# The filling of a scan pipeline: where the weights' means stand, which PSUM banks are used, and who computes chunk 11's taps

## The chip, the core and the metric

The kernel runs on one core of a Trainium2 chip. A core has five engines that run side by side and wait for each other by semaphores: TensorE (PE, matrix products), VectorE (DVE), ScalarE (ACT), GpSimd (POOL) and SyncE (SP, which here only issues DMA transfers). Each engine works through its own list of instructions in the order in which the program wrote them. The metric is the device time of one execution in microseconds, the median of several.

## What is computed

The input `x` has 2 images of 768 channels by 64 x 64 positions. Two layers follow each other, each added to its input. The change touches only the first layer, and of that only the start:

```python
x = x + mamba(_gn(x), ...)             # layer 0
x = x + attention(_gn(x), ...)         # layer 1

# layer 0
x  = hs @ in_proj_w.T                  # 768 -> 1536 channels
xs = conv3x3_depthwise(x) + conv_b
xs = xs * sigmoid(xs)                  # SiLU: "activations" below
dt, Bs, Cs = split(xs @ x_proj_w.T)
delta = softplus(dt @ dt_w.T + dt_b)
dA, dBu = exp(delta * A), delta * u * Bs
states = scan(dA, dBu)                 # along the 4096 positions, 4 states per channel
y  = sum_n(states * Cs) + D * u
y  = (y - mean) * rsqrt(var) * ln_g + ln_b
out = y @ out_proj_w.T
```

The last normalisation is folded into the output weights: each row of `out_proj_w.T` is multiplied by `ln_g` of its channel, and the mean of all the scaled rows is taken off. The kernel does that once, at its start, and keeps the result (`wo_dr`) in device memory.

## The kernel before

**Tiling.** The 1536 inner channels are 12 chunks of 128 (`KI`), the positions 16 tiles of 512 (8 per image, `NI` in all). The work of layer 0 is a list of 192 items (`NQ0` = 16 tiles x 12 chunks). One call of `step(g)` (L1162) writes out, in a fixed order, one item's worth of every stage. The stages run at different offsets: step g does the input projection of item n = g + 17 (`in_proj`), the convolution's taps of item a = g + 15 (`taps_dve`, `AHEAD` = 15), the scan of item g, and the output projection that lies 12 items behind (`out_proj`, `BEHIND`). The order is written by hand: the call stands inside `tc.manual_schedule()`, so each engine meets its instructions in just the order of the code.

**The filling.** Before the first scan (g = 0) there are 17 steps, g = -17 to -1, in which only the front stages run. The loop at L1333 counts sixteen of them as v = 0 to 15 (so n = v and a = v - 2), and the step g = -1 follows in the main loop. I call them step 0 to step 16, by n. Below, "projection 7" is `in_proj(7)`, that is step 7.

What one filling step v holds, engine by engine and in this order:

- SP: load the weights of projection v + 2 (`load_wi`, four buffers), one or two pieces of image 1 for its group statistics (`gn_load`), and later tiles of x.
- PE: one image row before the tile (`row0`, only for the first twelve), then the projection (`in_proj`, twelve matrix instructions into one PSUM bank), then what is appended at the end of the step (one tap by PE, `taps_pe`; x_proj of four chunks, `x_proj_pair`).
- DVE: the taps of chunk v - 2 (`taps_dve`, L436), one `scalar_tensor_tensor` each, into a PSUM accumulator `acc`; the last one writes the slot `u`. Then the pieces' statistics.
- ACT: copy of the row (L339), in every fourth step four SiLUs with a table load before and after (`silu`, L443), the centre tap of chunk v - 1 which starts its accumulator (`tap_act`, L390), the copy of projection v to the buffer `xs` (`in_proj_evict`, L364 to L367), the normalisation of the next tile (`norm_x`, L307), the products of two taps that are added by DMA (`taps_act`, L402).
- POOL: issues the two accumulating DMAs that add those tap products (`taps_dma_sum` L408, `taps_dma` L414).

Of the nine taps of a chunk the centre is ACT's, taps 0 and 2 go by DMA in three chunks of four, and in the filling's chunks 3, 7 and 11 tap 1 goes by PE instead, through a diagonal matrix (`diag`, L385, `taps_pe`, L422), and no tap by DMA. What remains is DVE's: six taps or seven.

**Buffers that order the work.** There is one accumulator bank (`psC`, "acc"), so the centre tap of chunk a + 1 waits until DVE has finished chunk a. There are two `xs` buffers, so the copy of projection n waits until DVE has finished chunk n - 2. The projections share one bank (`psA`), except the odd ones from 12 on (`po0`), so a projection waits for the copy of the one before it. The `u` slots come from a first-in first-out list of 46.

**The output weights.** `wg` holds all twelve chunks of `out_proj_w.T`, loaded in steps 2 to 5. Behind step 7 `out_weights_rows` (L256) multiplies them with `ln_g` and `ln_b` on PE, and behind step 8 `out_weights_mean` (L269 to L273) makes the mean row and the bias. From step 8 on each chunk is scaled by ACT (L276), the mean is taken off by POOL or DVE (L277), and one step later SP stores it (L280). The scale is written behind everything else of its step on ACT, and the subtraction likewise on its engine.

**The end of the filling.** x_proj of the tile's last four chunks comes in step 14, its two halves are added and copied in step 15 (`x_halves`, `x_sum`, `x_dbl`), and B and C go to device memory and come back spread over all partitions (`load_bc`, L470) in step 16. The softplus of the first two chunks and the exponentials of the first are ACT's in step 16. `bc`, `s`, the two `da` buffers and the `tm` buffers lie in a pool (`late`) that takes over the space of the pool with `wg`.

Of the kernel before, what the change touches and what calls it, by code (L numbers as in the profile page):

```python
# [14 lines left out]
P = 128  # L15
# [4 lines left out]
NS = 4  # L20
# [24 lines left out]

DMA_TAPS = ((0, 2, 6), (0, 2, 6), (0, 2, 6), (0, 2))
PE_TAPS = ((), (), (), (1, 7))
FILL_DMA_TAPS = ((0, 2), (0, 2), (0, 2), ())  # L50
FILL_PE_TAPS = ((), (), (), (1,))

AHEAD = 15
BEHIND = 12
# [13 lines left out]
def both_layers(  # L68
# [174 lines left out]


    def out_weights_load(wg, k):
        nc.sync.dma_start(wg[:, k : k + 3, :], out_wT[k * P : (k + 3) * P, :].rearrange("(k p) m -> p k m", p=P))

# [2 lines left out]
    def out_weights_rows(wg, rows):  # L252
        gb = psO.tile([P, 512], F32, tag="po0", name="pgb")
        for k in range(KI):
            for j in range(KM // 2):
                nc.tensor.matmul(  # L256
                    gb[32 * j : 32 * j + 2, :MG], pc[:, k, PC_G : PC_B + 1], wg[:, k, j * MG : (j + 1) * MG],
                    start=(k == 0), stop=(k == KI - 1),
                )
        for j in range(KM // 2):  # L260
            nc.scalar.copy(rows[32 * j : 32 * j + 2, :], gb[32 * j : 32 * j + 2, :MG])

    def out_weights_mean(rows, wmean, pick):
        pb = psS.tile([P, 512], F32, tag="st", name="pbo")
        wm = [psO.tile([P, 512], F32, tag=f"po{e}", name=f"pwm{e}") for e in range(2)]
        for j in range(KM // 2):
            for e in range(2):
                m = 2 * j + e
                nc.tensor.matmul(pb[:, m : m + 1], rows[:, e * P : (e + 1) * P], pick[:, j, P : P + 1], start=True, stop=True)  # L269
            nc.tensor.matmul(wm[j // 2][:, j % 2 * MG : (j % 2 + 1) * MG], pick[:, j, :P], rows, start=True, stop=True)  # L270
        nc.scalar.copy(wmean[:, : 2 * MG], wm[0])
        nc.scalar.copy(wmean[:, 2 * MG :], wm[1][:, :MG])
        nc.scalar.copy(bias_o, pb[:, :KM])  # L273

    def out_weights_scale(wg, wmean, k, engine):
        nc.scalar.activation(wg[:, k, :], wg[:, k, :], AF.Copy, scale=pc[:, k, PC_G : PC_G + 1])  # L276
        engine.tensor_sub(wg[:, k, :], wg[:, k, :], wmean)  # L277

    def out_weights_store(wg, k):
        nc.sync.dma_start(  # L280
            wo_dr[:, k // 3, :, k % 3, :].rearrange("q p m -> p q m"), wg[:, k, :].rearrange("p (q m) -> p q m", m=2 * P)
        )

    us, deltas, dus, sqs, tms = {}, {}, {}, {}, {}
# [58 lines left out]
    def in_proj(n):  # L343
        i, c, b, t = where(n)
        nn = TL if t < NT - 1 or b + 1 < NB else TL - W
        w = wis.pop(n)
        if KI <= n < AHEAD + 2 and n % 2:
            pa = psO.tile([P, 512], F32, tag="po0", name=f"pa{n}")
        else:
            pa = psA.tile([P, 512], F32, tag="psa", name=f"pa{n}")  # L350
        for k in range(KM):
            nc.tensor.matmul(pa[:, :nn], w[:, k, :], xts[i, k][:, :nn], start=(k == 0), stop=(k == KM - 1))  # L352
        pas[n] = pa
        give_w(w)
        if c == KI - 1:
            for k in range(KM):
                give(xts.pop((i, k)))
# [15 lines left out]


    def dma_taps(a):
        return (DMA_TAPS if a >= AHEAD else FILL_DMA_TAPS)[a % 4]

    def pe_taps(a):
        return (PE_TAPS if a >= AHEAD else FILL_PE_TAPS)[a % 4]

    def diag(a):
        c = a % KI
# [3 lines left out]
        dgs[a] = dg  # L386

    def tap_act(a):
        acc = psC.tile([P, 512], F32, tag="acc", name=f"acc{a}")
        nc.scalar.activation(  # L390
            acc.rearrange("p (h w) -> p h w", w=W), xs_bufs[a % 2][:, 1 : 1 + TR, 1 : 1 + W], AF.Copy,
            scale=pc[:, a % KI, PC_W + 4 : PC_W + 5],
        )
        accs[a] = acc
# [735 lines left out]
    with tc.manual_schedule():  # L1130
# [31 lines left out]
        def step(g, prep=None):  # L1162
# [46 lines left out]
            if 0 <= a + 1 < NQ0:  # L1209
                diag(a + 1)  # L1210

            do_silu = g % 4 == 1 and 0 < a <= NQ0
            do_soft = g % 2 == 1 and 0 <= g + 1 < NQ0
            if do_silu:
                nc.scalar.preload_act_table_set(SILU_SET)
                for q in range(4):
                    silu(a - 4 + q)
            if do_soft:
                nc.scalar.preload_act_table_set(SOFTPLUS_SET)
                softplus_pair(g + 1)  # L1220
            if do_soft or do_silu:
                nc.scalar.preload_act_table_set(EXPLN_SET)
            if 0 <= a + 1 < NQ0:
                tap_act(a + 1)
# [22 lines left out]
                    norm_x1(0, d[1] + 1, k)  # L1247
            if 0 <= a + 1 < NQ0 and dma_taps(a + 1):
                taps_act(a + 1)
            if 0 <= g - 3 < NQ0:  # L1250
                square(g - 3)

# [55 lines left out]
                prep()  # L1308
            if do_silu:
                for q in range(0, 4, 2):  # L1310
                    x_proj_pair(a - 4 + q)
            if v == len(by_step) + 1:
                gn_aggregate(1)
                norms[g + 2] = gn_finish(1)
# [5 lines left out]
                norms[g + 2][0][0]()  # L1320

        with tc.tile_pool(name="l0st", bufs=1, side="right") as sp:
            wg = sp.tile([P, KI, DM], F32, name="wg")
            rows = sp.tile([P, MG], F32, name="gb_rows")
            nc.vector.memset(rows, 0.0)
            wmean = sp.tile([P, DM], F32, name="wmean")
            pick = sp.tile([P, KM // 2, P + 1], F32, name="pick")
            nc.sync.dma_start(pick, pick_in)

            first = -AHEAD - 2  # L1330
            ready_w = {8: (0,), 9: (1, 2), 10: (3,), 11: (4, 5), 12: (6, 7), 13: (8, 9), 14: (10,), 15: (11,)}
            prep = {7: lambda: out_weights_rows(wg, rows), 8: lambda: out_weights_mean(rows, wmean, pick)}
            for v in range(AHEAD + 1):  # L1333
                if 2 <= v < 6:
                    out_weights_load(wg, 3 * (v - 2))
                step(first + v, prep.get(v))
                if v == 0:
                    nc.scalar.activation(neg_a, pc[:, :, PC_A : PC_A + NS], AF.Exp)
                    nc.scalar.mul(neg_a, neg_a, -1.0)
                for k, engine in zip(ready_w.get(v, ()), (nc.gpsimd, nc.vector)):  # L1340
                    out_weights_scale(wg, wmean, k, engine)
                for k in ready_w.get(v - 1, ()):
                    out_weights_store(wg, k)
            for k in ready_w[AHEAD]:
                out_weights_store(wg, k)

        late = right.enter_context(tc.tile_pool(name="l0l", bufs=1, side="right"))
        bc = late.tile([P, 2 * NS, TL], F32, name="bc")

        ysum = late.tile([P, 3, TL], F32, name="ysum")  # L1350
        tm_bufs = [late.tile([P, TL], F32, name=f"tm{j}") for j in range(5)]
        das = [late.tile([P, NS, TL + 1], F32, name=f"da{j}") for j in range(2)]
        for da in das:
            nc.gpsimd.memset(da[:, :, 0], 0.0)
        s = late.tile([P, NS, TL + 1], F32, name="s")
        for g in range(-1, NQ0 + 2):
            step(g)
        right.close()

# [199 lines left out]
```

## Time and profile before

| | us |
|---|---|
| median of 3 runs | 3741.39 (3737.32 to 3745.57) |
| the profiled execution, its own time | 3742.55 |
| its span, first to last instruction | 3740.6 |

| stretch of the profiled execution, us | length | PE busy | DVE busy | ACT busy | POOL busy |
|---|---|---|---|---|---|
| 0 to 212.09 (up to the first scan) | 212.09 | 151.92 | 147.03 | 92.58 | 40.70 |
| 212.09 to 361.77 (scan, no output projection yet) | 149.68 | 104.75 | 144.16 | 125.03 | 81.74 |
| 361.77 to 2700 (all stages) | 2338.23 | 2268.69 | 2231.61 | 1993.16 | 1348.41 |
| 2700 to the end (layer 1) | 1040.60 | 1021.55 | 345.06 | 354.45 | 305.27 |

A busy time near the length of its stretch marks an engine that hardly waits there. The profile gives busy times per stretch, the groups of instructions by line, a timeline of each engine with the idle time before an instruction and what ended it, and a list of who waited for whom.

### The profile page before, as it was taken

Reading aid. Unit: us, or ns where it says so; the run is one execution under the profiler, and the core shown is the slowest. Engines: PE = TensorE matmul, PEld = TensorE weight load, DVE = VectorE, ACT = ScalarE, POOL = GpSimd, SP = SyncE. Lnnn points to the kernel's source line nnn. Section 1 sums busy time; section 2 is a strip of 40 time slices with the busy share of each in tenths; the row PEclk is TensorE's granted clock in tenths of the full one; section 3 lists DMA queues with packets and bytes.
Section 4 is the critical chain, followed back from the end, with each engine's and each line's share of the span. In section 5 each row is a group of like instructions: output and inputs, shape, how many; then the busy total and the mean of one; then the engine's idle time right before and its main releaser. Section 6 shows DMA issues by size and latency. Waiting matters only on the chain. (4 is left out here: it accounts for less than half of the span.)

```text
span 3740.6 us, 37806 instructions
## 1 busy us (share of the span) xinstructions
PE 3546.9 (95%) x11098; PEld 1763.4 (47%) x11098; DVE 2867.9 (77%) x2614; ACT 2565.2 (69%) x4988; POOL 1776.1 (47%) x1809
## 2 busy tenths in 40 slices
PE   5877999999999999999999999999999999999999
PEld 3422333333333333333343333333346658886688
DVE  7699999999999999999999999997721362224522
ACT  2588888888888988888889888887633541244221
POOL 0245565555655555555555655554443314320232
PEclk9988999999999999999999999999999999999999
DMA  9677898889989899898889988897666628764487
GB/s 353 176 177 147 188 205 185 201 190 212 202 187 201 184 212 201 190 210 175 201 200 199 205 181 202 187 213 175 145 195 181 206 79 271 250 214 127 150 270 245
DMA packets 379725, 737.93 MB, mean 197 GB/s; under 512 B 44240, under 2 KB 116880, under 8 KB 375424
## 3 DMA queue, kind: packets, MB, share of 16 engines
q0 software_dynamic: 145632, 269.03, 42.1%
q1 hardware_dynamic: 233888, 466.49, 38.0%
q8 instruction: 90, 1.47, 0.2%
q14 instruction: 115, 0.94, 0.1%
HBM read 440.96 MB, written 60.03 MB: 134 GB/s over the span
## 5 line engine op out<-in xcount | busy, mean ns | idle before, releaser
L352 PE MATMUL pa<-u,w 128*128 128x512 f32 (+1 forms) x2304 | 1046.1, 604 | 19.3 <-ACT carry L367 14.7
L578 PE MATMUL po<-u,w 128*128 128x512 f32 x2256 | 1013.4, 599 | 16.9 <-DVE u L590 16.9
L514 DVE TENSOR_TENSOR_SCAN s<-da,s 128x2052 f32<-128x2052 f32 x192 | 851.1, 4433 | 19.5 <-ACT u L307 0.5
L352 PEld LDWEIGHTS pa<-u,w 128*128 128x128 f32 x2304 | 433.3, 193 | 617.6 <-issue 488.7
L578 PEld LDWEIGHTS po<-u,w 128*128 128x128 f32 x2256 | 420.1, 190 | 596.1 <-issue 549.4
L501 POOL TENSOR_TENSOR ysum<-da 128x1024 f32<-128x1024 f32 x192 | 384.6, 2003 | 588.4 <-DVE da L521 465.4
L436 DVE SCALAR_TENSOR_TENSOR acc<-xs,pc,acc 128x512 f32<-128x512 f32 x741 | 558.4, 754 | 41.5 <-PE acc L422 11.5
L489 ACT ACTIVATE da<-dl,neg_a 128x512 f32<-128x512 f32 x768 | 489.6, 713 | 0.0
L512 DVE TENSOR_TENSOR s<-du,bc 128x2048 f32<-128x2048 f32 x192 | 439.0, 2286 | 57.1 <-POOL du L493 55.4
L408 POOL DMA_DIRECT2D tm<-tm x309 | 267.9, 867 | 439.9 <-ACT tm L402 380.6
L521 DVE TENSOR_TENSOR da<-s,bc 128x2048 f32<-128x2048 f32 x192 | 440.1, 2292 | 6.3
L508 POOL DMA_DIRECT2D u<-ysum x384 | 378.5, 1249 | 4.5 <-issue 2.7
L390 ACT ACTIVATE acc<-xs,pc 128x512 f32<-128x512 f32 x192 | 132.3, 689 | 286.3 <-DVE u L436 285.0
L402 ACT ACTIVATE tm<-xs,pc 128x512 f32<-128x512 f32 x486 | 317.1, 717 | 3.6 <-DMA tm<-tm 3.0
L493 POOL TENSOR_TENSOR du<-dl,u 128x512 f32<-128x512 f32 x192 | 243.8, 1270 | 0.0
L414 POOL DMA_DIRECT2D u<-tm x177 | 205.1, 1159 | 53.6 <-issue 36.4
L861 PE MATMUL po_p<-v,w 128*128 128x256 f32 x672 | 171.9, 380 | 1.4 <-ACT po_p L958 1.4
L861 PE MATMUL po_p<-u,w 128*128 128x256 f32 x624 | 159.6, 379 | 0.0
L436 DVE SCALAR_TENSOR_TENSOR u<-xs,pc,acc 128x512 f32<-128x512 f32 x192 | 143.6, 748 | 9.5 <-DVE acc L436 0.4
L861 PE MATMUL acc_p<-u,w 128*128 128x256 f32 x556 | 143.7, 382 | 4.1 <-DMA w<-woutP 2.9
L477 PE MATMUL pz<-xd,dt_w 48*128 48x512 f32 x384 | 112.6, 664 | 36.5 <-DVE gs_x L193 14.9
L806 POOL TENSOR_TENSOR v<-u 128x256 f32<-128x256 f32 x21 | 15.7, 758 | 276.7 <-ACT u L824 262.5
(284 smaller groups left out, 4970.3 us busy)
## 6 DMA issues: line engine op xcount, KB each, us to landing
u<-ysum POOLq DMA_DIRECT2D x384, 256.0 KB, 5.8
tm<-tm POOLq DMA_DIRECT2D x309, 256.0 KB, 4.5
w<-in_wP SPq DMA_DIRECT2D x192, 384.0 KB, 5.0
w<-wo_dr SPq DMA_DIRECT2D x192, 384.0 KB, 4.8
u<-x SPq DMA_DIRECT2D x263, 256.0 KB, 4.8
w<-s_dr_p SPq DMA_DIRECT2D x288, 192.0 KB, 4.0
u<-tm POOLq DMA_DIRECT2D x177, 256.0 KB, 5.8
bc<-bc_dr SPq DMA_DIRECT2D x32, 1024.0 KB, 6.9
```

What stands on the lines that cost most here:

```text
L352: nc.tensor.matmul(pa[:, :nn], w[:, k, :], xts[i, k][:, :nn], start=(k == 0), stop=(k == KM - 1))
L402: nc.scalar.activation(tm.rearrange("p (h w) -> p h w", w=W), xs[:, dy : dy + TR, dx : dx + W], AF.Copy, scale=pc[:, c, PC_W + j : PC_W + ...
L408: nc.gpsimd.dma_start(tms[a][0], tms[a][q], accum_op=ALU.add)
L436: nc.vector.scalar_tensor_tensor(dst, xs[:, dy : dy + TR, dx : dx + W], pc[:, c, PC_W + j : PC_W + j + 1], acc, ALU.mult, ALU.add)
L489: nc.scalar.activation(das[g % 2][:, n, 1:], deltas[g], AF.Exp, scale=neg_a[:, c, n : n + 1])
L501: nc.gpsimd.tensor_add(ysum[:, 0 : 2 + g % 2 : 1 + g % 2, :], da[:, 0:2, 1:], da[:, 2:4, 1:])
L508: nc.gpsimd.dma_start(us[g], ysums(g, n), accum_op=ALU.add)
L512: nc.vector.tensor_mul(s[:, :, 1:], dus.pop(g).unsqueeze(1).to_broadcast([P, NS, TL]), bc[:, :NS, :])
L514: nc.vector.tensor_tensor_scan(sf, das[g % 2].rearrange("p n l -> p (n l)"), sf, 0.0, ALU.mult, ALU.add)
L521: nc.vector.tensor_mul(das[g % 2][:, :, 1:], s[:, :, 1:], bc[:, NS:, :])
L578: nc.tensor.matmul(po[e], w[:, kk, e * P : (e + 1) * P], us[i * KI + k], start=(k == 0), stop=(k == KI - 1))
L861: nc.tensor.matmul(dst, half[:, k, :], tiles[blocks[seq[i][0]][:3]][what][k], start=(start and k == 0), stop=(k == KH - 1), skip_group_che ...
```

## The change

1. **Banks.** In the filling the accumulators alternate between two banks (`psC` "acc" and `psS` "st"), and every odd projection goes to the bank "po1".
2. **Taps.** In the filling chunks 3 and 7 are treated like the others (taps 0 and 2 by DMA). Chunk 11 has all eight taps by DVE. No tap goes by PE and no diagonal is made.
3. **First activations.** The SiLUs of chunks 0 to 3 and 4 to 7 move from the steps with a = 4 and 8 to those with a = 5 and 9 (steps 7 and 11), and there behind everything else of ACT. Those of chunks 8 to 11 stay where they are.
4. **Means.** `out_weights_rows` and `out_weights_mean` both come at the end of step 12. Scaling follows in steps 12 to 15 (3, 4, 3, 2 chunks). POOL subtracts for 9 chunks in the same step, DVE for 3 chunks one step later.
5. **Four buffers and the order of the late pool.** `wg` is four tiles of three chunks. The late pool is laid out anew, so that `da0` and the `tm` buffers of step 16 no longer overlap `wg`, and `bc` overlaps only its first two tiles. `da1` is cleared behind step 16.

```diff
-FILL_DMA_TAPS = ((0, 2), (0, 2), (0, 2), ())
-FILL_PE_TAPS = ((), (), (), (1,))
+FILL_DMA_TAPS = (0, 2)
...
     def out_weights_mean(rows, wmean, pick):
-        pb = psS.tile([P, 512], F32, tag="st", name="pbo")
-        wm = [psO.tile([P, 512], F32, tag=f"po{e}", name=f"pwm{e}") for e in range(2)]
+        wm = psZ.tile([P, 2, 512], F32, tag="pz", name="pwm")
+        pb = wm[:, 1, MG : MG + KM]
...
-    def out_weights_scale(wg, wmean, k, engine):
-        nc.scalar.activation(wg[:, k, :], wg[:, k, :], AF.Copy, scale=pc[:, k, PC_G : PC_G + 1])
-        engine.tensor_sub(wg[:, k, :], wg[:, k, :], wmean)
+    def out_weights_scale(wg, k):
+        w = wg[k // 3][:, k % 3, :]
+        nc.scalar.activation(w, w, AF.Copy, scale=pc[:, k, PC_G : PC_G + 1])
+
+    def out_weights_sub(wg, wmean, k, engine):
+        w = wg[k // 3][:, k % 3, :]
+        engine.tensor_sub(w, w, wmean)
...
-        if KI <= n < AHEAD + 2 and n % 2:
-            pa = psO.tile([P, 512], F32, tag="po0", name=f"pa{n}")
+        if n < AHEAD + 2 and n % 2:
+            pa = psO.tile([P, 512], F32, tag="po1", name=f"pa{n}")
...
     def dma_taps(a):
-        return (DMA_TAPS if a >= AHEAD else FILL_DMA_TAPS)[a % 4]
+        return DMA_TAPS[a % 4] if a >= AHEAD else FILL_DMA_TAPS if a != KI - 1 else ()
     def pe_taps(a):
-        return (PE_TAPS if a >= AHEAD else FILL_PE_TAPS)[a % 4]
+        return PE_TAPS[a % 4] if a >= AHEAD else ()
+    def silu_of(a):
+        if a < KI:
+            return {5: 0, 9: 4}.get(a)
+        return a - 4 if a % 4 == 0 and a <= NQ0 else None
...
-        acc = psC.tile([P, 512], F32, tag="acc", name=f"acc{a}")
+        bank, tag = (psS, "st") if a < AHEAD and a % 2 == 0 else (psC, "acc")
+        acc = bank.tile([P, 512], F32, tag=tag, name=f"acc{a}")
...
-            do_silu = g % 4 == 1 and 0 < a <= NQ0
+            first4 = silu_of(a)
+            do_silu = first4 is not None
...
+            if do_silu and a >= KI:
+                silus()
...
             if 0 <= a + 1 < NQ0 and dma_taps(a + 1):
                 taps_act(a + 1)
+            if do_silu and a < KI:
+                silus()
+                nc.scalar.preload_act_table_set(EXPLN_SET)
...
-            wg = sp.tile([P, KI, DM], F32, name="wg")
...
+            wg = [sp.tile([P, 3, DM], F32, name=f"wg{q}") for q in range(KI // 3)]
-            ready_w = {8: (0,), 9: (1, 2), 10: (3,), 11: (4, 5), 12: (6, 7), 13: (8, 9), 14: (10,), 15: (11,)}
-            prep = {7: lambda: out_weights_rows(wg, rows), 8: lambda: out_weights_mean(rows, wmean, pick)}
+            scaled_w = {12: ((0, 1), (2,)), 13: ((3, 4, 5), (6,)), 14: ((7, 8), (9,)), 15: ((10, 11), ())}
+            def means():
+                out_weights_rows(wg, rows)
+                out_weights_mean(rows, wmean, pick)
...
-                step(first + v, prep.get(v))
+                step(first + v, means if v == 12 else None)
...
-                for k, engine in zip(ready_w.get(v, ()), (nc.gpsimd, nc.vector)):
-                    out_weights_scale(wg, wmean, k, engine)
-                for k in ready_w.get(v - 1, ()):
+                for k in sum(scaled_w.get(v, ((), ())), ()):
+                    out_weights_scale(wg, k)
+                for k in scaled_w.get(v, ((), ()))[0]:
+                    out_weights_sub(wg, wmean, k, nc.gpsimd)
+                for k in scaled_w.get(v - 1, ((), ()))[1]:
+                    out_weights_sub(wg, wmean, k, nc.vector)
+                for k in sum(scaled_w.get(v - 1, ((), ())), ()):
                     out_weights_store(wg, k)
...
-        bc = late.tile([P, 2 * NS, TL], F32, name="bc")
-        ysum = late.tile([P, 3, TL], F32, name="ysum")
-        tm_bufs = [late.tile([P, TL], F32, name=f"tm{j}") for j in range(5)]
-        das = [late.tile([P, NS, TL + 1], F32, name=f"da{j}") for j in range(2)]
-        for da in das:
-            nc.gpsimd.memset(da[:, :, 0], 0.0)
+        ysum = late.tile([P, 3, TL], F32, name="ysum")
+        bc = late.tile([P, 2 * NS, TL], F32, name="bc")
         s = late.tile([P, NS, TL + 1], F32, name="s")
-        for g in range(-1, NQ0 + 2):
+        da1 = late.tile([P, NS, TL + 1], F32, name="da1")
+        tm_bufs = [late.tile([P, TL], F32, name=f"tm{j}") for j in (0, 3, 1, 2, 4)]
+        tm_bufs = [tm_bufs[j] for j in (0, 2, 3, 1, 4)]
+        das = [late.tile([P, NS, TL + 1], F32, name="da0"), da1]
+        nc.gpsimd.memset(das[0][:, :, 0], 0.0)
+        step(-1)
+        nc.gpsimd.memset(das[1][:, :, 0], 0.0)
+        for g in range(NQ0 + 2):
             step(g)
```

## The prediction

> **What bounds the kernel.** I begin with the busy times per stretch (columns: stretch, length, then busy time and instructions of PE, PEld, DVE, ACT, POOL, then the TensorE clock granted, DMA share, GB/s).
>
> ```profile
> 100.00:120.00 20.00, 18.16 (x113) 7.78 (x111) 13.24 (x19) 10.25 (x19) 3.71 (x5) 1.00 0.76 190
> 160.00:180.00 20.00, 12.86 (x25) 5.35 (x24) 14.06 (x16) 6.28 (x11) 5.37 (x4) 0.83 0.72 197
> 240.00:260.00 20.00, 13.85 (x30) 5.81 (x31) 19.61 (x12) 16.89 (x32) 10.66 (x11) 0.83 0.81 158
> 440.00:460.00 20.00, 20.00 (x52) 8.03 (x51) 19.69 (x11) 19.92 (x41) 9.25 (x10) 1.00 0.98 228
> ```
>
> From 440 on PE is full: it is the bound of the long stretch. From 240 to 260 DVE is full. At 160 nobody is: an order of waits is the bound. The change touches only the last kind, before the first scan. DVE does that scan in its timeline here:
>
> ```profile
> 208.55 2.34 DVE L436 SCALAR_TENSOR_TENSOR acc<-xs,pc,acc 128x512 f32<-128x512 f32 x3 [5.10 <-ACT tm L402]
> 210.92 0.75 DVE L436 SCALAR_TENSOR_TENSOR u<-xs,pc,acc 128x512 f32<-128x512 f32 x1
> 212.09 2.29 DVE L512 TENSOR_TENSOR s<-du,bc 128x2048 f32<-128x2048 f32 x1 [0.42 <-DMA bc<-bc_dr]
> ```
>
> From 212.09 DVE idles for 5.5 us in 149.68, then PE takes over as bound at 361.77 and idles for 69.5 in 2338. So **what counts is when the multiplication at 212.09 starts**; whatever it gains, the end gains. The list of waits (100 to 420 us; total, times, longest) says what holds the filling:
>
> ```profile
> ACT acc L390 <- DVE u L436: 47.2, 18, 7.4
> DVE wg L277 <- ACT wg L276: 20.8, 4, 7.9
> PE acc L422 <- ACT acc L390: 11.8, 2, 7.1
> PE pa L352 <- ACT carry L367: 8.7, 6, 3.0
> DVE acc L436 <- PE acc L422: 8.1, 1, 8.1
> ```
>
> The first line is the single accumulator bank, the second DVE standing before a scaling that ACT reaches late, the third and fifth the tap by PE, the fourth the projections' single bank.
>
> **How I work it out.** I follow the engines' lists step by step; an instruction starts when the one before it has gone and what it needs has ended (plus 0.05 to 0.1 us, as between the rows). Pitches from the timelines: on PE a row 1.3, a projection 5.2 (its end 0.15 later), a pair of x_proj 0.93; on DVE a tap 0.79 (six: 4.7), a piece 0.6, a subtraction 2.1; on ACT a centre tap 0.62, a projection's copy 0.8, two tap products 1.2, four SiLUs with both table loads 5.2, a normalisation 0.7, a scaling 0.84, a softplus pair with its loads 3.9, four exponentials 2.5.
>
> At full clock these rules put the old kernel's first scan at 210.3, 1.8 too early. The clock is missing:
>
> ```profile
> 149.88 7.11 PE L352 MATMUL pa<-u,w 128*128 128x512 f32 x12 [1.96 <-ACT carry L367]
> 157.84 5.42 PE L352 MATMUL pa<-u,w 128*128 128x512 f32 x12 [0.84 <-ACT carry L367]
> 170.40 2.07 PE L422 MATMUL acc<-xs,dg 128*128 128x512 f32 x2 [7.14 <-ACT acc L390]
> ...
> 189.64 5.42 PE L352 MATMUL pa<-u,w 128*128 128x512 f32 x12
> ```
>
> In PE's timeline (start, length) the same twelve instructions take 7.11 behind an idle spell and 5.42 without, and the tap 2.07 instead of the 1.02 of step 8. The Trainium skill ("TensorE: Matmul & The Clock Gate", "What's actually happening") says that PE falls to half clock after an idle window of some 3.4 us and returns after a busy one. With windows of 3.4 us, one under half busy halving the next, the old first scan comes at 212.0. The rule isn't always kept: projection 15, at 189.64, takes 5.42 although PE had idled 2.69 before the x_proj ahead of it. I use it, because it speaks against the change, as seen below.
>
> **The banks.** Projections 3 to 7 no longer wait for the copy before them; row and projection follow each other every 6.5 us, as 61.60 to 68.09 already shows. DVE needs 5.3 or 5.9 per step and starts each chunk as the last one ends, since its centre tap was made meanwhile. Projection 7 starts at 101.9 instead of 109.61. That includes 5 us from the SiLUs of step 6, now gone from there.
>
> **The taps.** Chunks 3 and 7 lose a tap on DVE (0.8 each) and a PE tap, and gain two products on ACT (1.2) and two accumulating DMAs; chunk 11 gains a DVE tap (0.8) and loses the PE tap, whose wait of 7.14 at 170.40 goes. All but that lies in slack. The added DMAs fall where the DMA share is above 1.0 until 100 us. The skill ("Trainium Kernel Development and Optimization", "Key Constraints") says that all queues share the same 16 engines; the trace agrees: tap DMAs landed after 7 to 9 us there and after 3.5 later. POOL passes them one behind another, so u of chunk 3 lands at 110 to 113.6, and its SiLU would start at 112.4: 0 to 1.2 lost. I take 0.
>
> **The SiLUs last.** They begin in step 7 behind ACT's own work, at 109.2. But x_proj is at the end of PE's step and needs them: PE stands from 107.3 to 112, and row and projection 8 are queued behind. Projection 8 starts at 115.4 at full clock. In step 11 it is the same: PE stands from 141 to 147, and projection 12 is late. Both gaps hold a whole window, so by the rule x_proj and some of the projection run at half clock: 1 to 2 us in step 8 and 1 to 2 more in step 12. Without the rule these cost 0.
>
> **The means.** The weights' products with gain and bias (5.3) and the means (2.6) go from behind steps 7 and 8, where PE waits anyway, to behind projection 12, in the path. ACT copies between them (1.1), so projection 13 starts 9.2 after the end of 12, and ACT can't reach the centre tap of chunk 12 before the means are copied: DVE idles about 10 us there. This gives back most of what the first steps won.
>
> **Scalings and stores.** ACT has 12 scalings as before, now all in its fullest steps. DVE's subtractions come a step later and no longer wait (20.8 before). From the end of projection 13 ACT hardly waits, and I add it up: copy, products, four scalings 5.3; SiLUs, centre tap, copy, products, three scalings 10.3; halves, centre tap, x_dbl with its wait for PE, copy, products, two scalings 6.6; diagonals, softplus, centre tap, copy, products, exponentials 9.5. From 171.9 that ends at 203.6 (now 210.98). POOL's last subtraction ends at 197.5 (old: 203.43). SP then stores, loads one weight and asks for B and C at 198.5 (old: 206.38). Of this 2.0 is the wait for the last stores' landing, which `bc` no longer has. Landing takes 5.7 as now. The clearing of `da1` on POOL adds a wait for the last store, until 200.2, and du of item 0 is behind it; but that waits for the products of step 16 until 201 anyway.
>
> | start of | trace | old by the rules | new |
> |---|---|---|---|
> | projection 7 | 109.61 | 109.4 | 101.9 |
> | projection 8 | 121.63 | 121.2 | 116.7 |
> | projection 12 | 157.84 | 157.4 | 151.9 |
> | projection 13 | 172.27 | 171.7 | 166.6 |
> | projection 16 | 199.92 | 199.3 | 191.5 |
> | load of B and C | 206.38 | 206.3 | 198.5 |
> | first scan's multiplication | 212.09 | 212.0 | 204.2 |
>
> **The sum:** 204.2 - 212.1 = -7.9 us (the windows' phase moves it from 7 to 8.6). At full clock throughout it is 200.8, or -11.3. Against the profiled execution's 3742.55 that makes 3734.7; the median of the runs is 1.2 lower, so I say 3733.5. A measurement of this kernel can tell about 0.2% from no change, that is 7.5 us: my forecast lies just beyond that edge.
>
> **Rivals.**
>
> *Full clock (0.18).* The waits of 5 us don't bring half clock, as before projection 15. First scan near 201, time 3730.
>
> *The waits eat most of it (0.24).* The tap DMAs hop along POOL at 9 us each; if they still do at chunk 3, u lands 3 us after its SiLU is due, and PE waits with ACT. With one further cold window at step 12 and one at step 15, 5 of the 7.9 go: 3738.5. For it: the SiLU of chunk 2 waited 3.48 for such a DMA. Against it: the new SiLUs come a step later.
>
> *The long loop pays (0.10).* The four slots more that chunks 3 and 7 take turn the list of 46 slots, so every later tile lies in other slots. If a slot were then asked for before its last reader is through, PE would wait in each step. PE idles 0.38 us per step in the loop now; 0.085 more in 180 steps is 15.4, from where the kernel is slower than before beyond the edge. With 0.1 it is 3751.5. Against it: the list is first in, first out, and from step 17 on as many slots are free as before.
>
> *My forecast (0.48)*, own range 3730 to 3737.5; three in five of it lie beyond the edge. So faster 0.29 + 0.18 = 0.47, within 0.19 + 0.24 = 0.43, slower 0.10. The range takes in full clock and the eaten gain, not the loop: 3726 to 3746.
>
> **What would show it.** Right: projections 3 to 7 at a pitch of 6.5; PE idle 5 us before x_proj in steps 7 and 11 and groups of 6 to 7 us behind; no wait of DVE for a scaling; DVE idle some 10 us after chunk 11; the first scan at 204; the stretch from there to the end as long as now, 3528.5. Wrong: SiLUs waiting for a tap DMA; projections 3 to 6 waiting for weights; DVE idle more than 6 us in the 13 scan steps before the output projection starts; PE idle more than 75 us in the long loop.

## The result, and the profile after

The changed kernel takes 3742.34 us (median of 12 runs, 3739.91 to 3745.41), the kernel before in the same comparison 3741.69 (12 runs, 3736.08 to 3746.49): ratio 1.000, interval 0.9992 to 1.0008. The time is the same; the 8 us that I forecast did not come. It lies inside the whole range that I gave (3726 to 3746), but outside my forecast's own range (3730 to 3737.5). The profiled execution's own time is 3743.16, its span 3741.4.

First the busy times of the same four stretches as before (same columns):

```profile
100.00:120.00 20.00, 15.89 (x53) 8.17 (x52) 11.69 (x18) 11.12 (x20) 5.51 (x7) 0.83 0.82 204
160.00:180.00 20.00, 18.78 (x102) 9.31 (x93) 6.07 (x8) 10.16 (x19) 6.88 (x5) 0.91 0.29 92
240.00:260.00 20.00, 17.08 (x36) 7.11 (x36) 19.65 (x14) 14.73 (x28) 10.40 (x10) 0.75 0.80 170
440.00:460.00 20.00, 20.00 (x55) 8.06 (x54) 19.58 (x14) 19.93 (x41) 10.73 (x10) 1.00 0.96 229
```

At 240 DVE is still full and at 440 PE. At 160 PE is now busy (18.78 where it was 12.86) and DVE is not (6.07 where it was 14.06): PE works there on the weights' means and on projections 13 and 14, and DVE stands. The list of waits (100 to 420 us; total, times, longest) says the same:

```profile
ACT acc L401 <- DVE u L447: 23.2, 10, 5.1
DVE acc L447 <- ACT acc L401: 21.1, 6, 7.9
...
DVE wg L281 <- ACT wg L277: 14.5, 2, 12.2
```

The accumulator's line has halved (47.2 before), and both waits for the filling's PE tap are gone. But DVE now waits for centre taps, and once for 12.2 us before a subtraction. DVE's timeline at the end of the filling:

```profile
171.91 1.03 DVE L281 TENSOR_TENSOR wg<-wg,wmean 128x768 f32<-128x768 f32 x1 [12.20 <-ACT wg L277]
...
205.83 2.34 DVE L447 SCALAR_TENSOR_TENSOR acc<-xs,pc,acc 128x512 f32<-128x512 f32 x3 [6.65 <-PE acc L433]
208.20 0.75 DVE L447 SCALAR_TENSOR_TENSOR u<-xs,pc,acc 128x512 f32<-128x512 f32 x1
208.87 2.28 DVE L523 TENSOR_TENSOR s<-du,bc 128x2048 f32<-128x2048 f32 x1
```

The first scan's multiplication starts at 208.87, not at 204.2. It follows the taps of chunk 15 without a gap, and these had waited for PE. The load of B and C was hardly earlier: its first half, the only one that this multiplication reads, had landed at 208.4.

The table sets the milestones of all kernels side by side, from the start of each trace. "Items 119 to 122" is the time from the scan of item 119 to that of item 122, in the middle of the long loop; the experiment on the taps comes back to it. Start times of a projection that the trace merges with its neighbour are reckoned from the pitch. In late_scan three extra scans stand at 209.4, where the first scan would have come.

| kernel | projection 8 | projection 13 | load of B and C | first scan | items 119 to 122 | span |
|---|---|---|---|---|---|---|
| before | 121.6 | 172.3 | 206.4 | 212.1 | 40.2 | 3740.6 |
| before_again | 119.1 | 169.7 | 203.9 | 209.1 | 41.9 | 3743.3 |
| after | 117.3 | 168.2 | 203.1 | 208.9 | 45.1 | 3741.4 |
| after_again | 117.3 | 168.2 | 202.9 | 208.6 | 45.1 | 3748.6 |
| late_scan | 119.5 | 170.1 | 204.1 | 222.9 | 42.9 | 3752.5 |
| banks_only | 124.4 | 168.5 | 207.9 | 213.1 | 40.2 | 3741.6 |
| silus_first | 124.0 | 168.0 | 202.5 | 208.0 | 45.0 | 3738.9 |
| old_pool | 117.4 | 168.3 | 204.4 | 210.0 | 45.0 | 3744.2 |
| taps_back | 115.9 | 167.4 | 200.8 | 207.8 | 40.2 | 3735.0 |
| means_in_gaps | 115.5 | 155.7 | 189.0 | 197.1 | 44.7 | 3728.7 |
| spread | 115.2 | 162.9 | 184.6 | 200.0 | 44.7 | 3733.7 |
| scales_early | 115.5 | 155.7 | 186.9 | 193.5 | 45.1 | 3725.3 |
| scales_early_du | 114.9 | 155.9 | 187.0 | 192.6 | 45.0 | 3730.6 |
| subs_early | 115.9 | 156.0 | 181.6 | 190.7 | 45.0 | 3726.3 |

### The profile page after: what moved, and what is told of

It is laid out like the page before. It is cut to its first block, busy times and chain, and to the rows that moved or that the text cites. A ratio compares the mean times of both kernels' runs of the same rounds, so it can differ in the third digit from the quotient of the medians.

```text
span 3741.4 us, 37818 instructions
## 1 busy us (share of the span) xinstructions
PE 3545.8 (95%) x11092; PEld 1762.6 (47%) x11092; DVE 2867.9 (77%) x2612; ACT 2566.5 (69%) x4989; POOL 1781.8 (48%) x1814
## 5 line engine op out<-in xcount | busy, mean ns | idle before, releaser
L872 PE MATMUL po_p<-v,w 128*128 128x256 f32 x672 | 172.3, 380 | 1.4 <-ACT po_p L969 1.4
L369 ACT COPY xs<-pa 128x512 f32<-128x512 f32 (+1 forms) x192 | 109.7, 571 | 54.9 <-PE pa L356 48.8
```

The costliest lines, as they stand in the source:

```text
L872: nc.tensor.matmul(dst, half[:, k, :], tiles[blocks[seq[i][0]][:3]][what][k], start=(start and k == 0), stop=(k == KH - 1), skip_group_che ...
```

## The experiments

**The two kernels a second time.**

> The kernel before, unaltered, looked at a second time. It says how far the shift between two traces wanders when nothing differs. If shifts in the long loop are chance, the scans of this run should lie within 0.3 us of the first trace's up to the first scan, and then wander by 2 to 6 us through steps 20 to 190. If instead the loop is fixed by the program, they stay within 0.5 us to the end.

> The changed kernel, unaltered, a second time. Both theories: first scan's multiplication at 208.9 again, within 0.5 us. Theory that a shift of the first scan reaches the end: the median lies 3.2 us under the kernel before, within the 3 us that runs scatter. Rival, the long loop gives it back: equal to the kernel before, and the scans of step 130 and later at or behind those of before again.

Times: a single one for the kernel before, 3745.28; for the changed one 3743.57 against 3743.38 for the kernel before, ratio 1.000 (0.9991 to 1.0008). The changed kernel's first scan came again at 208.6, as expected, but not the 3.2 us of time. My expectation for the kernel before was wrong: its second trace puts the first scan 3 us earlier than the first one, not within 0.3, in DVE's timeline:

```profile
206.03 2.34 DVE L436 SCALAR_TENSOR_TENSOR acc<-xs,pc,acc 128x512 f32<-128x512 f32 x3 [5.11 <-ACT tm L402]
208.40 0.75 DVE L436 SCALAR_TENSOR_TENSOR u<-xs,pc,acc 128x512 f32<-128x512 f32 x1
209.06 2.28 DVE L512 TENSOR_TENSOR s<-du,bc 128x2048 f32<-128x2048 f32 x1
```

In the first trace projection 1 had come at 62.9, here at 61.1, and x_proj of step 6 waited 1.53 for a SiLU there and not at all here. So 212.09, the base of my sum, was one draw of something that varies by 3 us; a third trace, late_scan below, has 209.4. Against 209.1 the changed kernel, with 208.9 and 208.6, has gained next to nothing at the first scan. But both of its traces began late, as the first trace of before did (projection 1 at 62.7 and 62.8), and against that one it has gained 3.2 and 3.5. Two traces of each can't say which comparison is the fair one: the gain at the first scan lies between 0.2 and 3.5.

**Does a shift of the first scan reach the end?** Three extra scans on VectorE, whose results nobody reads, before the first one, in the kernel before (late_scan):

```diff
+            if g == 0:
+                for _ in range(3):
+                    nc.vector.tensor_tensor_scan(s..., das[0]..., das[0]..., 0.0, ALU.mult, ALU.add)
+                state_in(0)
```

> The kernel before, with three more scans of 4.43 us each written out on DVE ahead of the first scan, whose results nobody uses: the first scan comes 13 us late, and nothing else differs. Theory carry: the time is 13 us longer (11 to 16). Rival, the long loop takes up a shift of its start: less than 6 us longer.

Time 3755.06 against 3743.38, ratio 1.0031 (1.0019 to 1.0043): 11.7 us, with an interval of 7 to 16. The extra scans began at 209.41 and the first scan at 222.86, so the delay was 13.4. It goes to the end as far as these times can tell; the rival's "less than 6" is out.

**The means.** In means_in_gaps they go where PE waits for SiLUs anyhow: the products behind projection 7, the means behind projection 11. All else stays as in the change.

```diff
+            prep = {7: lambda: out_weights_rows(wg, rows), 11: lambda: out_weights_mean(rows, wmean, pick)}
...
-                step(first + v, means if v == 12 else None)
+                step(first + v, prep.get(v))
```

> The change with only the means put elsewhere: the weights' products with gain and bias behind projection 7, ahead of x_proj, and the mean row behind projection 11, ahead of x_proj, where PE stood idle 4.1 and 6.2 us in the changed kernel. If the means behind projection 12 are what the path paid for: projection 13 starts near 157 instead of 168.2, DVE idles 12 us less after chunk 11, and the first scan comes at 196 (195 to 199). Then theory carry: the time is 12 us under the changed kernel's and 15 under the kernel before. Rival, the long loop gives it back: less than 5 us under it though the first scan is 12 us earlier. Rival, the means weren't on the path: first scan later than 205.

Time 3731.33, ratio 0.9966 (0.9953 to 0.9978): 12.0 us less than before, and 12.2 less than the changed kernel in the same comparison (3743.57), with the first scan 11.6 earlier than in its trace there. PE's timeline, of the changed kernel first, then of this one:

```profile
101.61 5.37 PE L356 MATMUL pa<-u,w 128*128 128x512 f32 x12
111.08 4.29 PE L461 MATMUL px<-u,xp_w 128*64 128x512 f32 x8 [4.11 <-ACT u L454]
...
158.76 5.36 PE L256 MATMUL pgb<-wg,pc 128*2 128x256 f32 x72
165.34 0.61 PE L269 MATMUL pwm<-pick,gb_rows 128*128 128x1 f32 x4 [1.22 <-ACT gb_rows L261]
...
168.23 12.01 PE L356 MATMUL pa<-u,w 128*128 128x512 f32 x24
...
202.09 3.62 PE L433 MATMUL acc<-xs,dg 128*128 128x512 f32 x4 [2.46 <-issue]
```

```profile
106.62 5.36 PE L256 MATMUL pgb<-wg,pc 128*2 128x256 f32 x72
111.91 2.30 PE L461 MATMUL px<-u,xp_w 128*64 128x512 f32 x8
...
146.58 3.90 PE L461 MATMUL px<-u,xp_w 128*64 128x512 f32 x8 [3.58 <-ACT u L454]
150.41 15.72 PE L356 MATMUL pa<-u,w 128*128 128x512 f32 x36
```

In the changed kernel PE idles 4.11 in step 7 and does the products at 158.76, in the path. In the variant the products fill the same gap: x_proj starts only 0.83 later, and takes 2.30 instead of 4.29. Projections 12, 13 and 14 then follow without a break, 36 instructions in 15.72, and projection 13 starts 12.5 earlier. DVE waits 0.42 before its first subtraction instead of 12.20. So it was the place of the means that gave the gain back, as I had expected here. What stands last in the variant is the load of B and C:

```profile
197.07 2.29 DVE L523 TENSOR_TENSOR s<-du,bc 128x2048 f32<-128x2048 f32 x1 [3.89 <-DMA bc<-bc_dr]
```

**The banks alone**, in the kernel before (both accumulator banks, odd projections in "po1", the means' rows in the bank pair "pz"):

> The kernel before with only the banks of the change: accumulators alternating between two, the odd projections in a bank of their own, and the means in the third pair of banks. If the banks alone carry the early lead and the taps by PE and DVE's waits for scalings eat it: projection 5 at 89 to 90, projection 13 at 163 to 170 and the first scan 2 to 5 us before a kernel before of the same start (204 to 207). Rival, the banks are worth nothing without the other parts: 208.5 to 209.5.

Time 3743.98, ratio 1.000 (0.9991 to 1.0008), first scan 213.1: no gain at all, and later than both of my expectations. Projections 1 to 4 follow at the pitch of 6.5, but then ACT's and DVE's timelines show what that runs into:

```profile
104.78 1.33 ACT L445 ACTIVATE u<-u,pc 128x512 f32<-128x512 f32 x2 [6.38 <-DMA u<-u]
```

```profile
130.67 4.71 DVE L438 SCALAR_TENSOR_TENSOR acc<-xs,pc,acc 128x512 f32<-128x512 f32 x6 [11.41 <-PE acc L424]
148.80 2.18 DVE L278 TENSOR_TENSOR wg<-wg,wmean 128x768 f32<-128x768 f32 x1 [11.44 <-ACT wg L277]
```

The SiLUs of step 6 are reached before a tap DMA has landed, the PE tap of chunk 7 stands in PE's list behind projection 8, and DVE before a scaling. A faster stage only reaches the next wait sooner. The reverse, the changed kernel without the banks, was not tried, so what the banks are worth there stays open.

**The SiLUs first again**, in the changed kernel (with a = 4 and 8, ahead of ACT's other work):

```diff
-            return {5: 0, 9: 4}.get(a)
+            return {4: 0, 8: 4}.get(a)
...
-            if do_silu and a >= KI:
+            if do_silu:
```

> The changed kernel with the SiLUs of chunks 0 to 3 and 4 to 7 back in steps 6 and 10, ahead of ACT's other work. If moving them was worth something: the SiLU of chunk 3 waits for its tap DMA until 112, ACT and PE with it, projection 7 starts at 114 or later instead of 101.6, and the first scan comes 4 to 10 us later than in the changed kernel (213 to 219). Rival, PE's idle 4 and 6 us before x_proj were the larger cost: the first scan comes earlier than 208.

A single time, 3741.25, from which nothing follows; I read the trace. First scan 208.0. I had the waits right, and they are large (ACT's timeline, a SiLU each):

```profile
104.80 0.72 ACT L454 ACTIVATE u<-u,pc 128x512 f32<-128x512 f32 x1 [6.75 <-DMA u<-u]
110.86 0.72 ACT L454 ACTIVATE u<-u,pc 128x512 f32<-128x512 f32 x1 [5.34 <-DMA u<-u]
```

Projection 7 comes at 116.1 instead of 101.6. But projection 12 starts at 152.8, as in the changed kernel (152.6): x_proj of chunks 4 to 7 now idles 0.97 where it idled 6.21 in step 11, and the loss is made up. My expectation of a later first scan fell. The move of the SiLUs is worth nothing at the first scan, by this trace.

**The late pool and the four buffers.** old_pool has one `wg` tile and the old order of the late pool, all else as changed.

> The changed kernel with one weights buffer and the late pool laid out as before. If part 5 of the change frees nothing, because B and C wait for the last store either way: load of B and C at 203.1 and first scan at 208.9, both within 0.5. Rival, the layout is worth its 2 us: first scan at 210.5 or later.

A single time again, 3745.94; load of B and C at 204.4 instead of 203.1 and 202.9, first scan 210.0 instead of 208.9 and 208.6. This part is worth 1.1 to 1.4 us at the first scan, by one trace against two that began alike (projection 8 at 117.4 and 117.3): between my theory's nothing and the rival's 2 us.

**The taps.** taps_back treats chunks 3, 7 and 11 as before, all else as changed.

```diff
-FILL_DMA_TAPS = (0, 2)
+FILL_DMA_TAPS = ((0, 2), (0, 2), (0, 2), ())
+FILL_PE_TAPS = ((), (), (), (1,))
...
```

> The changed kernel, with chunks 3, 7 and 11 treated as before again (tap 1 by PE, no tap by DMA), everything else as changed. My theory: taps lie in slack, since the means behind projection 12 hold the filling; PE's tap of chunk 11 is 1 to 2 us in the path between projections 12 and 13, DVE gets 0.8 back. First scan's multiplication at 208 to 211 (changed kernel 208.9 and 208.6), time within 0.1% of the changed kernel. Rival: the waits of 7.14 and 8.1 us that the PE tap of chunk 11 had in the trace of before come back in full; first scan at 213 or later, time 3748 or more.

Time 3740.84 against 3742.85 for the kernel before, ratio 0.9996 (0.9987 to 1.0004); first scan at 207.8, a little ahead of what I had said. PE's old wait of 7.14 doesn't return. DVE's wait for the tap does, and is longer, but it costs nothing, since DVE would stand there anyhow; the wait before the subtraction behind it has shrunk from 12.20 to 6.14:

```profile
158.18 4.71 DVE L448 SCALAR_TENSOR_TENSOR acc<-xs,pc,acc 128x512 f32<-128x512 f32 x6 [13.14 <-PE acc L434]
```

The surprise is in the long loop: items 119 to 122 take 40.2 here and 44.7 to 45.1 in every kernel with the new taps, nine traces in all; the four others with the old taps take 40.2 to 42.9. The whole stretch from the first scan to the end agrees, though it scatters more: 3527.2 to 3534.3 in the five traces with the old taps (mean 3529.6; late_scan counted behind its extra scans), 3530.9 to 3540.0 in the nine with the new ones (mean 3534.3). POOL's timeline there, in taps_back and then in the changed kernel:

```profile
1774.05 1.26 POOL L505 TENSOR_TENSOR du<-dl,u 128x512 f32<-128x512 f32 x1
1775.26 0.86 POOL L420 DMA_DIRECT2D tm<-tm  x1
1775.84 2.05 POOL L520 DMA_DIRECT2D u<-ysum  x2
...
1785.03 2.00 POOL L513 TENSOR_TENSOR ysum<-da 128x1024 f32<-128x1024 f32 x1 [2.66 <-DVE da L533]
```

```profile
1778.33 1.26 POOL L504 TENSOR_TENSOR du<-dl,u 128x512 f32<-128x512 f32 x1
1780.99 0.88 POOL L419 DMA_DIRECT2D tm<-tm  x1 [1.40 <-ACT acc L401]
1781.57 2.07 POOL L519 DMA_DIRECT2D u<-ysum  x2
...
1791.77 2.00 POOL L512 TENSOR_TENSOR ysum<-da 128x1024 f32<-128x1024 f32 x1 [5.71 <-DVE acc L447]
```

With the new taps a tap DMA stands for 1.40 behind `du`, the accumulation of `ysum` behind it goes out just as a load of B and C begins (SP, 1782.38), and the next `ysum` waits 5.71 instead of 2.66. DVE's multiplication then waits 1.71 for `du` and its scan 0.47 more. One step later two small DVE operations of the group norm take 1.94 and 1.19 instead of 0.17 each, beside POOL's `ysum` and `du` that come just then; DVE's timeline, then POOL's:

```profile
1805.02 1.94 DVE L648 TENSOR_TENSOR msq<-mv,stats 128x6 f32<-128x6 f32 x1
1806.99 1.19 DVE L649 TENSOR_TENSOR msq<-msq 128x6 f32<-128x6 f32 x1
```

```profile
1804.93 2.00 POOL L512 TENSOR_TENSOR ysum<-da 128x1024 f32<-128x1024 f32 x1 [3.88 <-DVE mv L645]
1806.90 1.26 POOL L504 TENSOR_TENSOR du<-dl,u 128x512 f32<-128x512 f32 x1
```

Together these are 5.0, the whole difference between the two traces here. For the wait of 5.71 the list names DVE as the releaser; DVE had ended 1.9 before, and in five other traces the same wait is put down to the landing of `u<-ysum`. That the taps bring this is shown by the traces; the times, each against the kernel before (0.9996 and 1.000), have intervals that overlap, and do not show it by themselves. That they do so because they take four more `u` slots, so that later tiles lie elsewhere, was only argued: I did not try another number of slots.

**Scalings spread over steps 8 to 13**, with the means behind projections 7 and 8 (spread):

```diff
...
+    step(first + v, {7: lambda: out_weights_rows(wg, rows), 8: means_mid}.get(v))
...
+    scaled_w = {8: ((0, 1), ()), 9: ((2, 3), (4,)), 10: ((5, 6), ()), 11: ((7,), ()), 12: ((8, 9), (10,)), 13: ((11,), ())...}
```

> The changed kernel with the weights' products behind projection 7 (ahead of x_proj), the means behind projection 8, and the scalings spread over steps 8 to 13 (2, 3, 2, 1, 3, 1) instead of 12 to 15, so that ACT has none in steps 14 and 15. PE pays 2.6 for the means in step 8, where it is the bound; ACT loses five scalings of 0.84 in steps 14 and 15 and the stores end some 20 us before the first scan. If ACT's list and the last stores set the end of the filling: first scan's multiplication at 191 (189 to 194), five or six before means_in_gaps, and the time 16 to 18 us under the kernel before (ratio 0.9955). Rival, the load of B and C sets it whatever ACT does: 195 or later, and a time like means_in_gaps.

Time 3736.38 against 3743.53, ratio 0.9986 (0.9977 to 0.9994), first scan 200.0: less gain than I had said. The stores of scaled weights now stand in SP's list ahead of loads of x, for which ACT waited 3.44 in step 11. And the load of B and C, though asked for at 184.6, was not what decided. POOL's timeline:

```profile
196.92 0.86 POOL L425 DMA_DIRECT2D u<-u  x1 [10.72 <-issue]
...
198.06 1.95 POOL L504 TENSOR_TENSOR du<-dl,u 128x512 f32<-128x512 f32 x1
```

POOL stood 10.72 before the second accumulating tap DMA, which adds to what the first one wrote; that one had gone out at 185.22 and landed at 196.40. `du` of item 0, queued behind both, ended at 200.01; the multiplication followed at 200.04. From there came three more, each on top of means_in_gaps. **scales_early** moves nine scalings to steps 8 to 10 and leaves subtractions and stores; **scales_early_du** also writes `du` of item 0 ahead of that tap DMA; **subs_early** also subtracts and stores one step earlier (the three edits, one behind another):

```diff
+            early = {8: (0, 1, 2), 9: (3, 4, 5), 10: (6, 7, 8), 12: (9, 10, 11)}
...
+            if g == -1:
+                du(0)
...
-            scaled_w = {12: ((0, 1), (2,)), 13: ((3, 4, 5), (6,)), 14: ((7, 8), (9,)), 15: ((10, 11), ())}
+            scaled_w = {11: ((0, 1), ()), 12: ((2, 3, 4), (5,)), 13: ((6, 7), (8,)), 14: ((9, 10), (11,)), 15: ((), ())}
```

> The variant with the means in PE's gaps (products behind projection 7, mean behind projection 11; first scan at 197.1, ratio 0.9966), with nine of the twelve scalings moved to steps 8, 9 and 10, three in each, and the other three in step 12; subtractions and stores where they were. Theory: ACT's full steps 13 to 15 held bc's load back; without their nine scalings of 0.84 us the load is asked for at 183 to 185 (189.0), the first scan comes at 191 to 193, time about 3727. Rival: what counts is POOL's own queue, whose accumulating tap DMA of step 16 shares the transfer engines with that load, with du queued behind it, as in the spread variant (10.7 us stood there); then the first scan stays at 195 to 198 and the time at 3731.

> As the last one, and du of item 0 is written ahead of the tap DMAs of step 16 on POOL. If POOL's queue is what the first scan waits for, it comes 3 us or more earlier than without this edit, at 189 to 193, and the time is 3722 to 3727. If the load of B and C or ACT's exponentials decide, the edit changes the first scan by less than 1 us.

> As the last one (scalings early, du ahead of the tap DMAs; load of B and C asked for at 187.0, first scan at 192.6), with all subtractions one step earlier (steps 11 to 14 on POOL, none in step 15) and the stores with them. Theory: in the last runs ACT stood 3.8 us in step 16 and the load of B and C waited, both for POOL's last subtraction and the store behind it, which end only at 184.5 to 186.9; without them the load is asked for at 180 to 183, the exponentials end at 187, the first scan comes at 187 to 189.5, ratio about 0.995. Rival: the load then shares the transfer engines with other transfers and takes 9 us or more instead of 5.7 to 6.6, as in the spread variant, and the first scan stays at 191 or later.

Times 3728.01, 3729.32 and 3727.15, ratios 0.9964 (0.9950 to 0.9977), 0.9963 (0.9949 to 0.9976) and 0.9959 (0.9946 to 0.9973); the last one is against 3741.12, the others against 3742.85. The first scan moves from 197.1 to 193.5, 192.6 and 190.7. `du` did not decide here (0.9 us): the load did, in all three. In scales_early it was still held by POOL's last subtraction and the store behind it, and so was ACT:

```profile
186.95 1.33 ACT L413 ACTIVATE tm<-xs,pc 128x512 f32<-128x512 f32 x2 [3.82 <-issue]
```

In subs_early that wait is gone and the load goes out 5.4 earlier, but it lands 9.1 later instead of 5.7, so 2.0 remain. The load took the 9 us that my rival had said, and the first scan still came earlier, by 2.0 instead of the 3 to 5.6 of my theory. From means_in_gaps on, the times are the same within their intervals, though the first scan moves by 6.4: what these three bring to the time beyond means_in_gaps stays open. These four and spread are faster than the kernel before beyond their intervals, which the changed kernel is not. subs_early with the taps of before was not tried.

## Why the forecast of 3733.5 was wrong, and its range was not

- **"whatever it gains, the end gains"** held, within the noise, for late_scan's delay of 13.4 us and for means_in_gaps, whose first scan is 11.6 ahead of the changed kernel's and whose time is 12.2. My stretch of 3528.5 from the first scan to the end did not hold: it is 3532.5 in the changed kernel. Items 119 to 122 take 5.0 of it more, and the rest of the stretch gives 1.0 back.
- **The base.** "first scan's multiplication 212.09" was 3.0 and 2.7 later than in two other traces of the kernel before. Where the kernel before starts as in those, so much of the 7.9 is not there to be won.
- **The banks and steps 3 to 12** came as worked out: projections 3 to 7 at a pitch of 6.5, projection 7 at 101.6 (101.9 said), 8 at 117.3 (116.7), 12 at 152.6 (151.9). x_proj in steps 7 and 11 took 4.29 each behind idle spells of 4.11 and 6.21. The half clock behind them, which I charged with 1 to 2 us a step, was there (first two lines below) and cost 2.0 in x_proj, which takes 2.30 at full clock; the last SiLU waited 0.18 for its tap DMA, within the 0 to 1.2. The busy times by stretch, in which the third number from the end is the share of full clock that PE was granted, in the changed kernel:

```profile
111.10:115.30 4.20, 4.20 (x9) 1.37 (x9) 0.00 (x0) 3.16 (x4) 0.96 (x2) 0.50 0.49 83
148.40:152.60 4.20, 4.20 (x8) 1.24 (x8) 0.38 (x1) 3.98 (x6) 0.64 (x1) 0.50 0.74 125
168.20:171.60 3.40, 3.40 (x6) 1.46 (x5) 0.00 (x0) 3.12 (x6) 1.28 (x1) 0.54 0.00 0
202.10:205.50 3.40, 3.40 (x4) 1.48 (x5) 0.00 (x0) 3.14 (x7) 1.73 (x5) 0.51 0.87 266
```

  and in taps_back:

```profile
168.20:171.60 3.40, 3.40 (x9) 1.52 (x8) 0.58 (x1) 3.40 (x7) 2.17 (x2) 1.00 0.00 0
```

- **The means.** Their price behind projection 12, 9.2 by my sum, was 9.4. But the half clock came where I had not put it: projection 12 itself took 6.22 instead of 5.4, and the 24 instructions behind the means began at half clock (third line above) and took 12.01. In taps_back the same 24 took 10.46, at full clock throughout. With the 0.7 by which projection 12 began late, ACT's copy of projection 13 is 3.2 late (175.1 for 171.9). From there to its last exponential ACT took 31.8, and my sum had 31.7: the addition was right, its start was not. My windows, one under half busy halving the next, did not put it there. Why the clock fell there, and in taps_back with nearly the same instructions not, stays open.
- **"no longer wait"** for a scaling was wrong. DVE stood 12.20 before one, and 2.28 before another. I had booked that idle time as a wait for the centre tap of chunk 12, of some 10. That tap was ready at 172.5 and DVE's taps began at 172.9, so the subtraction cost little; the error was in the name of the wait.
- **"Of this 2.0 is the wait for the last stores' landing, which `bc` no longer has"** was wrong. SP's list of waits in the changed kernel, just before that load:

```profile
SPq L481 <- DMA wo_dr<-wg: 1.9, 1, 1.9
```

  Nor does the new pool free `da0` and the `tm` buffers, as the description of the change has it: in the addresses of the built kernel `da0` lies over the fourth `wg` tile and the `tm` buffers over the third. `bc` lies over the first tile alone, not over two, and the built program still lets its load wait for all of the last stores. ACT and POOL stood until 203.1 and 203.3. POOL's last subtraction, said for 197.5, ended at 199.95; with the 1.9 this makes nearly all of the 4.6 by which the load was late.
- **A term that the sum lacked.** It ended with the load and the exponentials. But chunk 15's taps on DVE need two taps by PE, which wait for ACT's centre tap behind the softplus. PE's started at 202.09 and took 3.62, at half clock (fourth line above), where means_in_gaps took 1.96; DVE's rest of the chunk took 3.0 more. In the changed kernel this chain was last, by half a microsecond: the load had landed at 208.4.

In short, between the two profiled executions: of the forecast 7.9 the terms of the filling took 4.7, which leaves 3.2 at the first scan (212.1 and 208.9), and the loop took 4.0, so that the changed kernel's span is 0.8 longer (3740.6 and 3741.4). The medians differ by 0.65 the same way. Traces of one kernel scatter by 3 us and more, though: the two of before are 212.1 + 3528.5 and 209.1 + 3534.3, so each of these terms is known to a few microseconds only.

That 3742.34 lies inside my range is luck as far as the path goes: I had widened the range for the rival "the waits eat most of it" (3738.5), and not for the long loop, where 4.0 went. That rival came nearest in time. Its waits for tap DMAs did not come, but its two further stretches at half clock did, one step later than it said (steps 13 and 16). My third rival named the slots, but as a price in every step of the loop, 15 us or more; PE idles 73.6 in the long loop, under the 75 that I had named as a sign, and the loss is at one place.

## What to carry to other kernels

Before you move work off a stage, find where its engine idles for another reason, and put it into that gap: the same 8 us of matrix work cost 12 us in the path and next to nothing in the gap. Take the parts of a change one at a time: here the SiLUs and the taps, undone, and the banks, alone, were worth about nothing at the first scan, and the taps cost 5 us in a place 1.6 ms later. Take a second trace of the kernel before, before a few microseconds of one trace become the base of a sum.

## What the runs showed of the hardware

- The accumulating tap DMAs landed, in the changed kernel, 3.3 us after issue at 119.7 (DMA share 0.74) and 6.2 to 9.5 us after issue from 70 to 100 (share 1.05), and 11.2 in spread beside the load of B and C (185.22 to 196.40), where the DMA share was 1.01. ACT waited 6.4 to 6.8 for one in step 6, POOL 10.7 in spread.
- The load of B and C is two transfers of 1 MB, and the first scan's multiplication reads the first. That multiplication began 5.7 us after the load was asked for in the first trace of before and in scales_early_du, 6.6 in scales_early, 8.0 in means_in_gaps and 9.1 in subs_early. What it shared the engines with was not varied.
- DVE's subtraction of 128 x 768 takes 0.94 us alone (twice in scales_early). Beside a run of three such subtractions on POOL it took 4.04 in the changed kernel and 5.45 in scales_early, and in both it ended 0.83 after POOL's run did, so it stood until POOL was through. POOL's timeline and DVE's, in the changed kernel:

```profile
178.02 5.63 POOL L281 TENSOR_TENSOR wg<-wg,wmean 128x768 f32<-128x768 f32 x3
```

```profile
180.44 4.04 DVE L281 TENSOR_TENSOR wg<-wg,wmean 128x768 f32<-128x768 f32 x1 [2.28 <-ACT wg L277]
```

  and in scales_early:

```profile
163.98 5.65 POOL L281 TENSOR_TENSOR wg<-wg,wmean 128x768 f32<-128x768 f32 x3
```

```profile
165.01 5.45 DVE L281 TENSOR_TENSOR wg<-wg,wmean 128x768 f32<-128x768 f32 x1
```

  The Trainium skill ("Trainium Architecture — The Big Picture", "What this means for kernel authors") says that DVE and GpSimd share a pair of ports under an exclusive lock; these rows agree with it. In the filling this lay beside the path. At items 119 to 122 DVE's small operations end with POOL's in the same way, within 0.1 us, and in the second trace of before too (one took 1.86, until 1805.11, POOL's `ysum` until 1805.08).
